# Rest rows of a gated MLP as pieces of the output stage, in an adaLN transformer block on one NeuronCore

## The chip, the core and the metric

The kernel runs on one core of a Trainium2 chip. Its engines work side by side: TensorE (PE, matrix products and transposes), VectorE (DVE), ScalarE (ACT), GpSimd (POOL) and SyncE (SP, which here only issues DMA transfers). Each engine takes its instructions in order, and so does each engine's queue of DMA issues. The metric is the device time of one execution in microseconds. Everything is float32.

## What is computed

One block with adaptive layernorm, for x of 2 batches x 1024 tokens x 1024 features, 32 heads of 32, and a gated MLP with 2752 inner rows:

```python
x = L0_attn_hidden_states
mod = (_silu(L0_c) @ L0_wmod).reshape(L0_c.shape[0], 6, 1, -1)
sa, ca, ga, sb, cb, gb = (mod[:, 0], mod[:, 1], mod[:, 2], mod[:, 3], mod[:, 4], mod[:, 5])
...
h = _layernorm(x, axis=-1) * (1 + ca) + sa
x = x + ga * _L0_attn_ref(h, L0_attn_Wqkv, ..., L0_attn_Wout)     # causal softmax with ALiBi
h = _layernorm(x, axis=-1) * (1 + cb) + sb
gate = jnp.einsum('bsh,ih->bsi', h, Wg) * ag
up = jnp.einsum('bsh,ih->bsi', h, Wu) * au
x = x + gb * (jnp.einsum('bsi,hi->bsh', jax.nn.silu(gate) * up, Wd) * ad)
```

## The kernel before

**Stages.** Modulation vectors and the layernorm of x; QKV projections of batch 0; attention of batch 0, then of batch 1, with dense products woven in; the rest of the output stage; gate and up; down. Large products are done with seven block products in place of eight (`seven`): the operands are sums of blocks, and what comes out is merged. For gate and up this is done at two levels, so the moving operands are sums T1 to T4 and blocks B11, B21, B22 of the second layernorm's output, over both batches, with inner sums of their own (`inner_b`, lines 1188 to 1202, four sums of 256 columns and four stores to `bop_dram`).

**Weaving.** `together(attention, dense_work(), share)` (line 1164) builds the program in the order in which the instructions will stand on each engine: it goes through attention's units (one block of scores, exponentials, products with V) and after each takes dense pieces until the planned microseconds of dense work reach `share(a)`. In batch 0's attention the dense work is the projections of batch 1, in batch 1's it is the output stage. The budgets are LEAD, DENSE0 and DENSE1 (line 1375).

**Output stage.** `output(b, js, ...)` (line 1285) goes pair by pair; a pair (b, j) is 256 tokens, j from 0 to 3. Its seven products of 4 matmuls 128x512 each use two PSUM banks in turn; VectorE and GpSimd gate them and add x. Then x1 is stored, the layernorm is done (`normalize`), four groups of transposes (`turned`, line 861) go through the `Todo` list, and h2, the transposed result, goes to DRAM. The list is worked off between the products of the next pair (from product `q0` on) and after them, and takes a bank of `banks.others`, which in attention is one bank.

**Rest rows.** Five stages of 512 rows leave inner rows 2560 to 2751. `rest_rows` (line 1396) does these 192 rows for each pair: three products of 8 matmuls with 256 columns (128 gate rows; 128 up rows; the last 64 of both in one), then Silu on ScalarE, one fused VectorE operation for the product with up, and a store to `rest_dram`.

**Between attention and gate** (lines 1558 to 1611): batch 0's h2 comes back from DRAM (`fetch`); rest rows of all eight pairs are done in twos, woven with the last transposes and with the output stage of pairs (1,2) and (1,3); `second(j)` makes the operands that need both batches: T1, T2, B22 on VectorE and T3, T4 on GpSimd. T3 and T2 share the tile `oo`.

**Gate and up.** Each of five stages (`for s in range(NSB)`) has seven entries (STAGES), each of seven block products into banks `gx`, `ux`, `gy`, `uy`. GpSimd makes the sums of weights (`gate_inner`, line 1700, and `gate_sums`, line 1691). `after(n, go)` (line 1737) puts work at a count of chain entries. `second_batch(3)` is made here (line 1744).

Of the kernel before, what the change touches and what calls it, by code (L numbers as in the profile page):

```python
# [18 lines left out]
P = 128  # L19
# [461 lines left out]
def kernel(  # L481
# [233 lines left out]

    last_exp = [None]
# [159 lines left out]
    class Todo:  # L876
# [18 lines left out]
        def add(self, go):  # L895
            self.list.append(go)

        def run(self, n, all_=False):
            self.place()
            for _ in range(min(n, len(self.list))):  # L900
                if not all_ and not self.banks.fresh():
                    return
                self.list.pop(0)(self.banks.turn())
                yield TURN
# [380 lines left out]
    def output(b, js, pools, banks, bt, todo, keep, q0=1):  # L1285
# [9 lines left out]
        for j in js:  # L1295
# [44 lines left out]
            for m in range(2):  # L1340
                for g in range(2):
# [10 lines left out]
                    todo.add(go)  # L1352

    def second_batch(j, pool, h0, h1):


        oo = pool.tile([P, 2, KC // 2, 2, P], FP, tag="oo", name=f"oo_{j}")
        t1, t4, lo1, hi1 = h0[:, 0 : KC // 2], h0[:, KC // 2 :], h1[:, 0 : KC // 2], h1[:, KC // 2 :]
        t2, t3 = oo[:, 0], oo[:, 1]
# [15 lines left out]
    LEAD, DENSE0, DENSE1 = 16.0, 370.0, 136.0  # L1375
# [20 lines left out]
    def rest_rows(pairs, rest_w, pool, psp, tiles):  # L1396

        n1 = REST[1][1]
        ib = 4 * NSB
        for b, j in pairs:  # L1400
            hl = tiles[b, j].rearrange("p k h t -> p k (h t)")
            ps = []
            for r in range(3):
                bank = psp.tile([P, 512], FP, tag="rp", name=f"rest_{b}_{j}_{r}")[:, 0:256]
                for k in range(KC):
                    matmul(bank, rest_w[r][:, k, :], hl[:, k, :], start=(k == 0), stop=(k == KC - 1))
                ps.append(bank)
                yield 3.4
            sg = pool.tile([P, 2, 256], FP, tag="rsg", name=f"rsg_{b}_{j}")
            ac = pool.tile([P, 2, 256], FP, tag="rac", name=f"rac_{b}_{j}")  # L1410
            nc.scalar.activation(sg[:, 0], ps[0], AF.Silu, scale=vt[:, R_AG + ib : R_AG + ib + 1])
            nc.scalar.activation(
                sg[64 : 64 + n1, 1], ps[2][0:n1], AF.Silu, scale=vt[0:n1, R_AG + ib + 1 : R_AG + ib + 2]
            )
            nc.vector.scalar_tensor_tensor(
                ac[:, 0], ps[1], vt[:, R_AU + ib : R_AU + ib + 1], sg[:, 0], ALU.mult, ALU.mult
            )
            nc.vector.scalar_tensor_tensor(
                ac[64 : 64 + n1, 1], ps[2][64 : 64 + n1],
                vt[64 : 64 + n1, R_AU + ib + 1 : R_AU + ib + 2], sg[64 : 64 + n1, 1], ALU.mult, ALU.mult,  # L1420
            )
            nc.sync.dma_start(rest_dram[0][:, b, j], ac[:, 0].rearrange("p (h t) -> p h t", h=2))
            nc.sync.dma_start(
                rest_dram[1][0:n1, b, j], ac[64 : 64 + n1, 1].rearrange("p (h t) -> p h t", h=2)
            )
# [93 lines left out]
    def dense_work():  # L1519
# [22 lines left out]
        out_args.extend((opools, banks, bt, Todo(banks), keep))  # L1542
        yield from output(0, range(NJ), *out_args)
        right["w"] = rest_weights(rwp, nc.sync)
# [15 lines left out]
    opools, _, bt, todo, _ = out_args  # L1560
# [5 lines left out]
    rps = rest_st.enter_context(tc.tile_pool(name="rest_ps", bufs=4, space=PSUM))  # L1566
# [7 lines left out]
    def rows(*pairs):  # L1574
        return rest_rows(pairs, rest_w, rest_pool, rps, kept)

# [4 lines left out]
    def with_turns(rows_):  # L1581

        together(rows_, todo.run(len(todo.list), True), lambda a: 0.16 * (a - 9.0))

    fetch(0, 0, nc.scalar)
    rest_w = right["w"]
# [7 lines left out]
    def between():  # L1594
        yield from rows((0, 1))
        second(0)
        yield from rows((1, 1))
# [472 lines left out]
```

## Time and profile before

| | |
|---|---|
| median of 3 executions | 2857.35 us (2853.57 to 2857.75) |
| the profiled execution's own time | 2851.89 us |
| its span, first to last instruction | 2850.2 us |
| granted TensorE clock, mean | 0.983 |
| batch 0's attention | about 388 to 901 us |
| batch 1's attention, first score block to last product with V | 901.4 to 1334.6 us |
| products of pair (1,2), start; of pair (1,3), end | 1382.98, 1454.93 us |
| last transposes of pair (1,3), end | 1480.2 us |
| gate, first product; end of stage 1 | 1501.43, 1553.35 us |

The span is cut into stretches by what TensorE works on. In a line of the windows the first number after the stretch is its length; then come the busy time of each engine with its instructions, the granted clock, the share of the DMA engines that is busy and what they move. A line of the waits names the waiting engine and tile, what the wait ended on, the sum, the number and the longest. A line of the timeline is start, length, engine, line, operation, output and input with their shapes, and in brackets the idle time ahead of it with what ended it. The chain of waits follows the last instruction back to what released it.

### The profile page before, as it was taken

What the parts mean: (1) busy time and instruction counts of PE and PEld (TensorE: products, weight loads), DVE (VectorE), ACT (ScalarE), POOL (GpSimd) and SP (SyncE); (2) the same over time, 40 slices, a digit from 0 to 9 for tenths busy, and PEclk for the clock granted to TensorE, in tenths of its full rate; (3) what the DMA queues carried; (4) which work ended last, traced back from release to release, by engine and by line L of the source; (5) the groups of instructions that cost most, each with busy time, mean ns of one, the idle gap of its engine ahead of it and who ended that gap; (6) DMA issues with size and microseconds to landing.
All of it is one profiled execution on the core that took longest, in us unless ns stands there. A gap on an engine that the chain in (4) does not pass through costs nothing. (4 is left out here: it accounts for less than half of the span.)

```text
span 2850.2 us, 29927 instructions
## 1 busy us (share of the span) xinstructions
PE 2698.4 (95%) x10271; PEld 1329.8 (47%) x10271; DVE 1454.4 (51%) x2285; ACT 685.5 (24%) x1523; POOL 1292.9 (45%) x1270
## 2 busy tenths in 40 slices
PE   7999999999999888889899999999999998999998
PEld 2444433333333222223664444444444447888776
DVE  5766525566634456656654453544535345443442
ACT  1322243444443556554111010110101101000000
POOL 3311124545565665655447474455636431322342
PEclk9999999999999899999999999999999999999999
DMA  9878873766755554433687576675866669554552
GB/s 348 301 278 296 293 241 107 237 225 201 233 157 191 155 172 137 149 123 113 198 295 252 162 265 195 192 271 162 272 183 229 201 190 279 150 148 137 167 143 79
DMA packets 377573, 579.14 MB, mean 203 GB/s; under 512 B 21590, under 2 KB 278712, under 8 KB 366276
## 3 DMA queue, kind: packets, MB, share of 16 engines
q1 hardware_dynamic: 363928, 556.12, 60.3%
q10 hardware_dynamic: 13484, 21.02, 2.3%
q8 instruction: 84, 1.38, 0.2%
q14 instruction: 77, 0.63, 0.1%
HBM read 411.89 MB, written 165.17 MB: 202 GB/s over the span
## 5 line engine op out<-in xcount | busy, mean ns | idle before, releaser
L1085 ACT ACTIVATE p<-sc,kw 128x128 f32<-128x128 f32 (+3 forms) x1024 | 421.6, 513 | 357.8 <-PE sc L763 341.7
L763 PE MATMUL bank<-wT,a 128*128 128x512 f32 x768 | 359.9, 613 | 12.0 <-DVE wT L832 6.8
L1117 POOL TENSOR_TENSOR p<-p,p 128x1024 f32<-128x1024 f32 (+3 forms) x128 | 262.4, 2050 | 174.6 <-PE av L763 142.6
L1117 DVE TENSOR_TENSOR p<-p,p 128x1024 f32<-128x1024 f32 (+3 forms) x192 | 250.2, 1314 | 142.8 <-POOL p L1089 85.0
L763 PE MATMUL bank<-wB,a 128*128 128x512 f32 x576 | 262.2, 601 | 1.2 <-DVE raw L984 0.6
L763 PE MATMUL sc<-cq,ck 32*128 32x512 f32 (+3 forms) x1536 | 192.9, 542 | 55.1 <-ACT p L1085 54.9
L763 PEld LDWEIGHTS bank<-wT,a 128*128 128x128 f32 x768 | 142.5, 195 | 189.8 <-issue 172.7
L1089 POOL TENSOR_SCALAR_AFFINE_SELECT p<-p 128x256 f32<-128x256 f32 x256 | 136.0, 544 | 196.2 <-ACT p L1085 192.5
L763 PE MATMUL av<-p,cv 128*32 128x512 f32 (+3 forms) x1536 | 170.6, 511 | 4.0 <-POOL p L1089 4.0
L763 PEld LDWEIGHTS bank<-wB,a 128*128 128x128 f32 x576 | 104.8, 190 | 144.3 <-issue 125.6
L763 PEld LDWEIGHTS sc<-cq,ck 32*128 32x128 f32 x1536 | 64.6, 186 | 192.2 <-ACT p L1085 106.3
L1842 PE MATMUL gy<-bt,sig 128*128 128x512 f32 x280 | 132.5, 596 | 10.9 <-DMA bt<-bop_B 6.0
L1842 PE MATMUL gx<-bt,sig 128*128 128x512 f32 x280 | 131.6, 592 | 0.0
L1842 PE MATMUL uy<-bt,siu 128*128 128x512 f32 x280 | 131.6, 592 | 0.0
L1842 PE MATMUL ux<-bt,siu 128*128 128x512 f32 x280 | 131.6, 592 | 0.0
L763 PEld LDWEIGHTS av<-p,cv 128*32 128x32 f32 x1536 | 33.8, 110 | 123.6 <-issue 81.5
L1842 PEld LDWEIGHTS gy<-bt,sig 128*128 128x128 f32 x280 | 52.4, 190 | 81.2 <-issue 71.3
L1842 PEld LDWEIGHTS uy<-bt,siu 128*128 128x128 f32 x280 | 53.2, 190 | 66.9 <-issue 66.0
L1842 PEld LDWEIGHTS gx<-bt,sig 128*128 128x128 f32 x280 | 53.2, 190 | 66.9 <-issue 66.1
L1842 PEld LDWEIGHTS ux<-bt,siu 128*128 128x128 f32 x280 | 53.2, 190 | 66.9 <-issue 65.0
L1842 PE MATMUL gx<-bt,wgS 128*128 128x512 f32 x160 | 75.2, 592 | 0.0
L1842 PE MATMUL ux<-bt,wuS 128*128 128x512 f32 x160 | 75.2, 592 | 0.0
(415 smaller groups left out, 4449.2 us busy)
## 6 DMA issues: line engine op xcount, KB each, us to landing
bt<-bop_T SPq DMA_DIRECT2D x140, 512.0 KB
bt<-bop_B SPq DMA_DIRECT2D x99, 512.0 KB
a<-hop SPq DMA_DIRECT2D x20, 1792.0 KB
wm<-in_L_wmod_dram SPq DMA_DIRECT2D x48, 512.0 KB
wB<-in_L_attn_Wqkv_dram SPq DMA_DIRECT2D x21, 1024.0 KB
aq_S<-act_S SPq DMA_DIRECT2D x16, 1280.0 KB
qk<-qs SPq DMA_DIRECT2D x16, 1024.0 KB
act_S<-asS SPq DMA_DIRECT2D x30, 512.0 KB
```

The lines of the kernel that those rows point to most:

```text
L763: return in_order(nc.tensor.matmul(*args, **kw_))
L1085: last_exp[0] = nc.scalar.activation(p[:, g, lo:hi], sp[:, g, lo:hi], AF.Exp, bias=kw[:, d, h_ : h_ + 1])
L1089: last_mask[0] = nc.gpsimd.affine_select(out=p[:, :, 0:P], in_=p[:, :, 0:P], pattern=[[0, 2], [1, P]], compare_op=ALU.is_ge, fill=0.0, bas ...
L1117: adders[b](half, jb).tensor_add(dst, dst, ps[half][:, :, 0:n])
L1842: nc.tensor.matmul(ps.rearrange("p (j t) -> p j t", j=NJ), ins[mat][qa][:, c2, :], bt[:, :, c2, :], start=(q in ("P1", "P2", "P5") and c2 ...
```

## The change

Rest rows are no longer a routine of their own after attention. `output` gets the rest weights and puts, behind a pair's transposes, three product pieces and two pieces without a planned cost (the activations) on its Todo list. In batch 1 the list is worked off from the sixth product on. DENSE1 rises from 136 to 190. Silu becomes g / (1 + exp(-g)), with the exponential on ScalarE (scale from the new constant `nag`) and the rest on VectorE; the up rows go through the constant-pool tile `sc`. Behind attention, three more PSUM banks join the shared one, batch 0's h2 is fetched on SP's queue, `second(0)` is done before the products of pair (1,2) and `second(1)` after those of (1,3); the operands of pairs 2 and 3 are both made in gate's first stages. T3 is made in place of the lower half of batch 1's h2, and `oo` holds T2 alone, in two buffers.

```diff
+    nag = const.tile([P, 2], FP, name="nag")
+    nc.vector.tensor_scalar_mul(nag, vt[:, R_AG + 4 * NSB : R_AG + 4 * NSB + 2], -1.0)
...
-        def add(self, go):
-            self.list.append(go)
+        def add(self, go, us=TURN):
+            self.list.append((go, us))
         def run(self, n, all_=False):
             self.place()
-            for _ in range(min(n, len(self.list))):
+            while n and self.list:
+                go, us = self.list[0]
+                if us is None:
+                    go()
+                    self.list.pop(0)
+                    continue
                 if not all_ and not self.banks.fresh():
                     return
-                self.list.pop(0)(self.banks.turn())
-                yield TURN
+                self.list.pop(0)
+                go(self.banks.turn())
+                n -= 1
+                yield us
...
-    def output(b, js, pools, banks, bt, todo, keep, q0=1):
+    def output(b, js, pools, banks, bt, todo, keep, q0=1, rest=None):
...
                     todo.add(go)
+            if rest is not None:
+                rest_pieces(b, j, todo, h2, *rest)
     def second_batch(j, pool, h0, h1):
-        oo = pool.tile([P, 2, KC // 2, 2, P], FP, tag="oo", name=f"oo_{j}")
+        t2 = pool.tile([P, KC // 2, 2, P], FP, tag="oo", name=f"oo_{j}", bufs=2)
         t1, t4, lo1, hi1 = h0[:, 0 : KC // 2], h0[:, KC // 2 :], h1[:, 0 : KC // 2], h1[:, KC // 2 :]
-        t2, t3 = oo[:, 0], oo[:, 1]
+        t3 = lo1
...
-    LEAD, DENSE0, DENSE1 = 16.0, 370.0, 136.0
+    LEAD, DENSE0, DENSE1 = 16.0, 370.0, 190.0
...
-    def rest_rows(pairs, rest_w, pool, psp, tiles):
...
+    def rest_pieces(b, j, todo, h2, rest_w, pool):
+        n1 = REST[1][1]
+        hl = h2.rearrange("p k h t -> p k (h t)")
+        tiles = {}
+        def product(w, bank):
+            ps = bank[:, 0:256]
+            for k in range(KC):
+                matmul(ps, w[:, k, :], hl[:, k, :], start=(k == 0), stop=(k == KC - 1))
+            return ps
+        def gate(ps, r, lo):
+            g, e = (pool.tile([P, 256], FP, tag=nm, name=f"{nm}_{b}_{j}_{r}") for nm in ("rg", "re"))
+            ib = R_AG + 4 * NSB + r
+            nc.scalar.activation(e[lo], ps[lo], AF.Exp, scale=nag[lo, r : r + 1])
+            nc.vector.tensor_scalar_mul(g[lo], ps[lo], vt[lo, ib : ib + 1])
+            tiles[r] = g, e
+        def act(r, lo, n):
+            g, e = tiles[r]
+            nc.vector.tensor_scalar(e[lo], e[lo], FAR, 1.0, ALU.min, ALU.add)
+            nc.vector.reciprocal(e[lo], e[lo])
+            nc.vector.tensor_mul(g[lo], g[lo], e[lo])
+            nc.vector.tensor_mul(g[lo], g[lo], urow[lo])
+            nc.sync.dma_start(rest_dram[r][0:n, b, j], g[lo].rearrange("p (h t) -> p h t", h=2))
+        every, lo, hi = slice(0, P), slice(0, n1), slice(64, 64 + n1)
+        urow = sc.rearrange("p k c -> p (k c)")
+        ib = R_AU + 4 * NSB
+        def up(bank):
+            nc.vector.tensor_scalar_mul(urow, product(rest_w[1], bank), vt[:, ib : ib + 1])
+        def last(bank):
+            ps = product(rest_w[2], bank)
+            gate(ps, 1, lo)
+            nc.scalar.activation(urow[lo], ps[hi], AF.Identity, scale=vt[hi, ib + 1 : ib + 2])
+        todo.add(lambda bank: gate(product(rest_w[0], bank), 0, every), 3.5)
+        todo.add(up, 3.5)
+        todo.add(lambda: act(0, every, P), None)
+        todo.add(last, 3.5)
+        todo.add(lambda: act(1, lo, n1), None)
...
+        out_args.append(1)
+        out_args.append((rest_weights(rwp, nc.sync), rwp))
         yield from output(0, range(NJ), *out_args)
-        right["w"] = rest_weights(rwp, nc.sync)
+        out_args[5] = 5
         yield from output(1, range(NJ // 2), *out_args)
...
-    rps = rest_st.enter_context(tc.tile_pool(name="rest_ps", bufs=4, space=PSUM))
+    rps = rest_st.enter_context(tc.tile_pool(name="rest_ps", bufs=1, space=PSUM))
+    banks.others = banks.others + [rps.tile([P, 512], FP, tag=f"rq{i}", name=f"rq{i}") for i in range(3)]
...
-    fetch(0, 0, nc.scalar)
-    rest_w = right["w"]
-    fetch(1, 0, nc.scalar)
     operands(1, NJ // 2, opools[1], wide)
     operands(1, NJ // 2 + 1, opools[1])
+    fetch(0, 0)
+    fetch(1, 0)
+    alone(todo.run(len(todo.list), True))
     fetch(0, 1)
-    with_turns(rows((0, 0), (1, 0)))
     fetch(1, 1)
-    def between():
-        yield from rows((0, 1))
-        second(0)
-        yield from rows((1, 1))
-    together(
-        between(), output(1, range(NJ // 2, NJ), *out_args, 3), lambda a: 0.6 * OUT_US / 2 * a / 20.6
-    )
-    in_range(rest_pool, rps)
+    second(0)
+    alone(output(1, range(NJ // 2, NJ), *out_args))
+    alone(todo.run(4, True))
     fetch(0, 2)
     second(1)
+    in_range(rest_pool, rps)
     fetch(0, 3)
-    with_turns(rows((0, 2), (1, 2)))
-    second(2)
-    alone(rows((0, 3), (1, 3)))
+    alone(todo.run(len(todo.list), True))
...
-            on_dve, on_pool = second_batch(3, pair_pool, kept[0, 3], kept[1, 3])
-            for go in on_dve[:2] + on_pool[:2]:
-                go()
-            for n, go in zip((8, 9, 12), on_dve[2:]):
+            on_dve, on_pool = [], []
+            for j in (2, 3):
+                d, p = second_batch(j, pair_pool, kept[0, j], kept[1, j])
+                for go in d[:2] + p[:2]:
+                    go()
+                on_dve += d[2:]
+                on_pool += p[2:]
+            for n, go in zip((2, 5, 6, 8, 9, 12), on_dve):
                 after(n, go)
-            for n, go in zip((10, 11), on_pool[2:]):
+            for n, go in zip((3, 4, 10, 11), on_pool):
                 after(n, lambda go=go: (go(), None)[1])
```

More of the change, by code (lines that the diff above doesn't have):

```diff
@@ L1394, in rest_weights @@
         return w
-    def rest_rows(pairs, rest_w, pool, psp, tiles):
+    def rest_pieces(b, j, todo, h2, rest_w, pool):
         n1 = REST[1][1]
[L1399 to L1413, printed above, removed]
-            )
[L1415 to L1425, printed above, removed]
@@ L1559 @@
     att.close()
-    opools, _, bt, todo, _ = out_args
+    opools, _, bt, todo = out_args[:4]
     pair_st = ctx.enter_context(ExitStack())
@@ L1572, in fetch @@
         eng.dma_start(kept[b, j], h2_dram[b][j])
-    def rows(*pairs):
-        return rest_rows(pairs, rest_w, rest_pool, rps, kept)
     def second(j):
@@ L1579, in second @@
             go()
-    def with_turns(rows_):
-        together(rows_, todo.run(len(todo.list), True), lambda a: 0.16 * (a - 9.0))
-    fetch(0, 0, nc.scalar)
-    rest_w = right["w"]
-    fetch(1, 0, nc.scalar)
     operands(1, NJ // 2, opools[1], wide)
     operands(1, NJ // 2 + 1, opools[1])
+    fetch(0, 0)
+    fetch(1, 0)
+    alone(todo.run(len(todo.list), True))
     fetch(0, 1)
-    with_turns(rows((0, 0), (1, 0)))
     fetch(1, 1)
-    def between():
-        yield from rows((0, 1))
-        second(0)
-        yield from rows((1, 1))
-    together(
-        between(), output(1, range(NJ // 2, NJ), *out_args, 3), lambda a: 0.6 * OUT_US / 2 * a / 20.6
-    )
-    in_range(rest_pool, rps)
+    second(0)
+    alone(output(1, range(NJ // 2, NJ), *out_args))
+    alone(todo.run(4, True))
     fetch(0, 2)
     second(1)
+    in_range(rest_pool, rps)
     fetch(0, 3)
-    with_turns(rows((0, 2), (1, 2)))
-    second(2)
-    alone(rows((0, 3), (1, 3)))
+    alone(todo.run(len(todo.list), True))
     ost.close()
```

## The prediction

> **What bounds the kernel now.** I read the page's busy times first, then the windows of the stages that the edit touches, the waits of TensorE in them, the timeline and last the chain of waits.
>
> ```profile
> PE 2698.4 (95%) x10271; PEld 1329.8 (47%) x10271; DVE 1454.4 (51%) x2285; ACT 685.5 (24%) x1523; POOL 1292.9 (45%) x1270
> ```
>
> TensorE bounds the whole kernel, so the questions are where it idles and whether the edit fills that idle time. The windows: batch 0's attention, batch 1's, two stretches of the output stage behind attention, the rows and transposes behind it, the first two gate stages.
>
> ```profile
> core 0: us, PE busy (x) PEld busy (x) DVE busy (x) ACT busy (x) POOL busy (x), PEclk, DMA share, GB/s
> 388.00:901.00 513.00, 496.41 (x2321) 185.55 (x2320) 271.07 (x412) 220.20 (x517) 260.20 (x267) 0.99 0.59 190
> 901.00:1335.00 434.00, 374.67 (x2174) 120.72 (x2176) 256.82 (x357) 241.70 (x580) 271.05 (x248) 0.94 0.48 149
> 1335.00:1383.00 48.00, 41.75 (x169) 29.71 (x170) 30.00 (x61) 4.58 (x9) 16.36 (x11) 0.96 0.70 216
> 1383.00:1455.00 72.00, 67.62 (x210) 37.72 (x209) 37.44 (x64) 9.63 (x15) 40.36 (x36) 1.00 0.74 239
> 1455.00:1501.00 46.00, 43.46 (x208) 37.49 (x207) 24.24 (x52) 8.45 (x12) 18.03 (x18) 1.00 0.82 277
> 1501.00:1553.00 52.00, 49.12 (x115) 21.41 (x114) 23.89 (x34) 5.66 (x11) 48.67 (x67) 1.00 0.78 245
> ```
>
> Batch 1's attention leaves TensorE idle for 434.0 - 374.7 = 59.3 us; behind attention, 1335 to 1501, it idles for 13.2 us of 166. Its waits in 901 to 1335:
>
> ```profile
> engine line waited for: us in total, times, longest us
> PE sc L763 <- ACT p L1085: 45.6, 42, 3.8
> PE bank L763 <- DVE h2t L869: 4.5, 1, 4.5
> ```
>
> The idle time is scores waiting for ScalarE's exponentials, in short pieces. Already one wait is for the VectorE eviction of the one PSUM bank that transposes share.
>
> The timeline has one pair's rest rows, and a reciprocal of 128 columns:
>
> ```profile
> 1348.49 10.52 PE L763 MATMUL rest<-hl,restw 128*128 128x256 f32 x48
> 1345.46 0.95 DVE L1138 RECIPROCAL rc<-rc 128x128 f32<-128x128 f32 x1 [2.88 <-DMA rc<-sum]
> ```
>
> The 48 records are one pair's 3 products of 8 matmuls, two records to a matmul: 10.35 us from start to start for a pair, 3.45 a product.
>
> The chain of waits ahead of gate, and POOL just ahead of the T3, T4 operands:
>
> ```profile
> 1463.98 6.13 DMA actr<-rac
> 1476.09 6.86 DMA bop_T<-inner_T
> 1492.21 4.93 DMA actr<-rac
> 1497.88 3.72 PE rest L763 x16
> ...
> 1510.41 2.35 POOL L1368 TENSOR_TENSOR hl<-hl,oo 128x1024 f32<-128x1024 f32 x1
> 1532.52 0.72 POOL L1698 TENSOR_TENSOR wuS<-wuA,wuS 128x256 f32<-128x256 f32 x1
> ```
>
> (The first four are the chain, the last two the timeline.) Stores and POOL operations set the order here, and rest rows are what TensorE does meanwhile.
>
> **What the Trainium skill says.** "ScalarE: Activation LUTs", What ACT_TABLE_LOAD costs: about 1283 ns for a load plus about 1380 ns of drain. The trace has loads of 1.28 us each; it does not show the drain apart. "VectorE: DVE Perf Modes", First, the fixed hardware budget: Reciprocal is an iterated divide with a repeat count of 8. The trace agrees in kind: 0.95 us beside 0.27 for a tensor_tensor of the same 128 columns. "SBUF — State Buffer", Who interferes with whom: a VectorE operation with two SBUF inputs contends with a GpSimd one that reads SBUF, for the whole instruction. The trace: 256-column operand sums of 0.41 us on VectorE, one taking 4.20 us at 1531.37 while POOL ran.
>
> **The change, part by part.**
>
> *Matmuls moved, none removed.* This and the places below are from the order of the built program. Rest rows are 8 x 10.35 = 83 us before and after. Of them (0,0) to (0,3), 12 products or 41.4 us, go into batch 1's attention. DENSE1 190 also asks for pair (1,1)'s last six half products there (10.3 us). Pairs (1,0) to (1,3) stay behind attention.
>
> *What they cost inside attention.* I measured the units of batch 1's attention, from one score block to the next. At 512 columns: 3.36 us with no dense piece (14 units), 4.38 with a 1.72-us piece (16), 5.38 with a piece and a transposition or settlement (14), 5.61 with two pieces (3). At 256: 2.40, 3.55, 5.47 with none, one and two. So a 1.72-us piece costs 1.0 to 1.15, a 3.45-us one 2.25 to 3.1. I take 2.6: 12 x 2.6 = 31, plus 6 x 1.05 = 6: **+37**. From below: if all 59.3 us of gaps were usable it would be nothing, but the gaps average 1.1 us each (45.6 in 42), so a 3.45-us product can't sit in one: at least 12 x 1.2 = 15. From above: nothing hidden is 51.7, and shared-bank waits like the 4.5 above can go past it.
>
> *VectorE.* A pair's activation was two 0.48-us operations, 0.97. Now: two multiplications out of PSUM (0.45 each), two min/add (0.25, from 0.22 for 128 columns), two reciprocals of 256 columns, four products (0.41, as the sums above) and `up` (0.45). The reciprocal is bounded by 0.95 (no more than 128 columns) and 1.9 (twice), and I take 1.9: 0.9 + 0.5 + 3.8 + 1.64 + 0.45 = 7.3. Four pairs add 29 us in attention, where none of it ran: 256.8 of 434 becomes 286 of 471, 61%. On average hidden behind TensorE; but VectorE runs in order, and the next piece needs its eviction, which I leave in the upper bound. Behind attention the same 7.3 stands between transposes and their bank; three added banks lighten that.
>
> *ScalarE's table loads* (seven between 1355 and 1465, 9 us) leave. ScalarE is busy 4.6 of 48 and 9.6 of 72 us there, so this is worth at most the 1.28 us on the chain at 1461.66: nothing on its own, since TensorE has rows to do.
>
> *From the end of batch 1's attention (1334.6) to the last transposes (1480.2).* Before: 145.6 us = 48.4 to the first product of pair (1,2), 72.0 for the two last pairs' products and two rows, 25.2 to the last transposition. After: the tail of (1,1), 13.9, is gone; its layernorm still takes the 13.7 from 1348.5 to the transposition at 1362.2, covered by 10.35 of rest (1,0); four transposes (0.66, with evictions about 7 in all), 10.35 of rest (1,1), and 7 for waits in the one bank with VectorE's evictions: about 39. Then 14 products x 3.44 = 48.2 plus about 5 for the transposes between them: 53. Then rest (1,2), 10.35, and four transposes: 14.6. Sum 107: **-38** (from -42, all waits gone, to -28).
>
> *From the last transposition to the end of gate's stage 1* (before: 1480.2 to 1553.35, 73 us, with 20.7 of rows ahead of gate). Ten us of rows leave. But a wait is added. second_batch(3), and now (2), run in gate's opening; T3, T4 are made in place, so POOL's T3 of pair 3 (`h2t_1_3`) must follow rest (1,3). POOL runs in order, and ahead of it stand 16 gate_inner operations, 32 gate_sums and hl_0_3: 48 x 0.683 + 2 x 2.35 = 37.5 us with itself (POOL was 94% busy in 1501 to 1553 already, and none of it can begin before the transposes free xr). SP's store bop_T3 waits for it, and behind that on SP stand T3, T4, B22, a bt load and last the rest store actr_1 of pair (1,3): ten issues of about 0.5, and 5 us for its landing (4.93 in the chain). ScalarE's first eviction of gate, whose tile takes the closed rest pool's space, waits for that store. Behind it on ScalarE stand all evictions of the stage, and TensorE's third chain entry waits for that bank. So entry 3 starts about 37.5 + 5 + 5 + 0.6 = 48 after the transposes, and from there to stage 1's end is 1508.3 to 1553.35 = 45 in the trace before, some 3 of it stalls that the later start covers: 48 + 42 = 90 against 73, **+17**. From below 0 (SP passes earlier and gate is bound by rows, whose 10 us then gain up to -10); from above +27, if weight loads queue behind.
>
> *New const, `nag`*: one small VectorE operation under the start's loads, 0.17 us without that cover. Fetches on SP rather than ScalarE: four issues of 0.5 in a queue that is waited for; in the bounds.
>
> **Sum.** 37 - 38 + 17 = +16. The profiled execution before took 2851.9 (span 2850.2 and 1.7 around it), so 2868; it lies 5.5 under the median of 2857.35, so as a median **2874**.
>
> **The rivals.**
> 1. *TensorE's gaps take the products* (other side). With VectorE and ScalarE at some 60%, products start while scores wait: 42 waits, 45.6 us. At an extension of 15, the sum is 15 - 38 + 17 = -6: 2851. It decides from an extension of 21 down. Against it: units with a piece are all longer. Chance 0.17.
> 2. *The wait at gate's start is short.* POOL or SP gets through, so gate starts some 12 us after the transposes: 37 - 38 - 5 = -6, 2851; if both, 2830. Chance 0.15. Against it: the counts above, and 48.67 of 52 us busy.
> 3. *VectorE and the shared bank bound attention.* Rest products, transposes and settlements all take one bank, and each waits for an in-order eviction: 12 x 4.5 = 54, sum 54 + 6 - 38 + 17 = +39, 2896. Chance 0.14.
> 4. *It does nothing:* 0 with opposite parts, inside 0.2%: about 2857.
>
> **How the numbers follow.** 0.2% is 5.7 us, about what can be told from no change. Likeliest case 0.54, its own range +5 to +32 (2862 to 2889), one in ten of it in the same band; rivals 1 and 2 together 0.32, of which some two thirds end faster than 5.7 under and most of the rest the same; rival 3 0.14. That gives faster 0.21, same 0.13, slower 0.66. Range 2846 to 2900: below it lies both good cases at once, above it bank waits and gate loads together.
>
> **What would show it.** Right: batch 1's attention 465 to 475 us long with TensorE busy above 88%; last attention product to last transposes about 107; ScalarE's first gate eviction ended by the store actr<-rg, and TensorE idle some 15 to 25 us in gate's third entry. Wrong: attention under 450, or no idle at gate's start, or waits for bank2's evictions above 20 us in attention.

## The result, and the profile after

The changed kernel takes 2905.78 us, median of 4 runs (2901.09 to 2910.17), beside 2855.46 us for the kernel before on the same chip: a ratio of 1.0169, with a 95% interval of 1.0149 to 1.0189. It is 50 us slower. The forecast was 2874 with a range up to 2900: right in its direction, 32 us too low, and the result lies outside the range.

The profiled execution has a span of 2908.4 us, 58.2 over that of before. The busy times on its page:

```profile
PE 2699.0 (93%) x10271; PEld 1331.4 (46%) x10271; DVE 1504.4 (52%) x2358; ACT 681.6 (23%) x1524; POOL 1291.8 (44%) x1270
```

TensorE's instructions are as many and its busy time the same within 1 us; VectorE has 50 us more. All that was lost is idle time of TensorE. The windows of the changed kernel, cut where those of before were cut: batch 1's attention; to the first product of pair (1,2); to the end of pair (1,3)'s products; to gate; gate's first two stages. ("Stage" is used here, as in the prediction, for one of the seven entries of STAGES, counted from 0, so the end of stage 1 is the end of the second. An "entry" of gate, the third or the seventh, is one of the seven block products in the first of them.)

```profile
core 0: us, PE busy (x) PEld busy (x) DVE busy (x) ACT busy (x) POOL busy (x), PEclk, DMA share, GB/s
897.00:1374.00 477.00, 423.13 (x2381) 159.99 (x2384) 290.72 (x402) 248.19 (x592) 268.61 (x251) 0.95 0.44 138
1374.00:1412.00 38.00, 29.46 (x138) 22.62 (x138) 27.22 (x63) 3.01 (x8) 4.71 (x4) 0.96 0.64 186
1412.00:1488.00 76.00, 51.17 (x124) 22.72 (x123) 45.51 (x69) 4.92 (x10) 48.35 (x38) 0.87 0.72 223
1488.00:1531.00 43.00, 28.35 (x119) 23.27 (x118) 32.75 (x62) 2.39 (x6) 22.57 (x23) 0.84 1.00 347
1531.00:1610.00 79.00, 49.88 (x114) 21.90 (x113) 27.55 (x47) 8.53 (x13) 48.44 (x63) 0.83 0.55 172
```

In attention TensorE idles for 53.9 us of 477, before for 59.3 of 434: it was given 49 us more to do, and only 5 of them came out of idle time. In the four windows behind it, TensorE idles for 77 us of 236; before it was 16 of 218. The granted clock has fallen there from 1.00 to between 0.83 and 0.87 in three of them.

By the anchors of the table of before (the first score block at 897.3, the last product with V at 1374.4, the last transposes' end at 1515.8, the end of gate's stage 1 at 1610.2):

| | before | forecast | measured |
|---|---|---|---|
| start of batch 1's attention | 901.4 | 0 | -4.1 |
| its length | 433.2 | +37 | +43.9 |
| from its end to the last transposes | 145.6 | -38 | -4.2 |
| from there to the end of stage 1 | 73.0 | +17 | +21.4 |
| sum | | +16 | +57.0 |

(The remaining 1.2 us of the span's 58.2 lie behind stage 1.) The earlier start is no gain of the change: in three runs below that differ from one another only behind attention (before_exp, exp_store_on_act, exp_pool_order) batch 1's attention starts at 891.9, 898.5 and 903.0 us. So stretches are compared by their length. One row holds 34 of the 41 us that were missed; attention holds 7, the stretch behind the transposes 4, and the early start gives 4 back. The waits of TensorE in batch 1's attention:

```profile
PE sc L766 <- ACT p L1096: 26.7, 27, 3.8
PE bank L769 <- DVE h2t L872: 9.7, 8, 2.7
PE bank L769 <- DVE rs L1138: 7.4, 2, 6.2
PE bank L766 <- issue: 4.1, 1, 4.1
```

And its three longest waits from the end of attention to the end of stage 1:

```profile
PE gx L1864 <- issue: 29.1, 1, 29.1
PE bank L766 <- DVE oP L1338: 21.9, 1, 21.9
PE rq L769 <- ACT sc L1449: 5.9, 1, 5.9
```

In attention the waits for exponentials fell from 45.6 to 26.7 us, and the waits of tile `bank` rose from 9.7 to 25.6 us, 21.2 of them in these lines. Behind it two single waits make 51 us.

**The wait of 29.1 us** is the forecast one, at gate's third entry. The changed kernel's timeline there, GpSimd, then SP, ScalarE and TensorE:

```profile
1554.66 2.34 POOL L1380 TENSOR_TENSOR h2t<-h2t 128x1024 f32<-128x1024 f32 x1
...
1557.03 1.57 SPq L1211 DMA_DIRECT2D bop_T<-h2t  x3
...
1561.99 0.45 SPq L1435 DMA_DIRECT2D actr<-rg  x1
...
1566.54 0.59 ACT L1663 COPY g_P<-gx 128x512 f32<-128x512 f32 x1 [31.51 <-DMA actr<-rg]
1567.22 3.61 PE L1864 MATMUL gx<-bt,sig 128*128 128x512 f32 x4 [29.12 <-issue]
```

T3 of pair 3 ends 41 us after the transposes (37.5 were worked out), the last rest store is issued 5 us later, and ScalarE's first gate eviction ends its wait 4.5 us after that.

**The wait of 21.9 us** was in no step of the forecast. The same kernel between the first and the second product of pair (1,3):

```profile
1438.96 3.60 PE L766 MATMUL bank<-wB_o,aoA 128*128 128x512 f32 x8
...
1456.66 0.42 DVE L1205 TENSOR_TENSOR inner_T<-hl 128x256 f32<-128x256 f32 x1 [6.03 <-POOL inner_T L1208]
1457.12 0.50 SPq L1314 DMA_DIRECT2D xr<-_attn_hidden_states_dram  x1
1460.14 0.43 DVE L1205 TENSOR_TENSOR inner_T<-oo 128x256 f32<-128x256 f32 x1 [1.92 <-DMA bop_T<-inner_T]
1462.45 1.26 POOL L1342 TENSOR_TENSOR xr<-xr,oP 128x512 f32<-128x512 f32 x1 [5.81 <-DMA xr<-_attn_hidden_states_dram]
1463.74 0.69 DVE L1338 TENSOR_TENSOR oP<-ga,bank 128x512 f32<-128x512 f32 x1 [2.05 <-POOL xr L1342]
1464.48 5.51 PE L766 MATMUL bank<-wB_o,aoA 128*128 128x512 f32 x8 [21.92 <-DVE oP L1338]
```

VectorE's eviction of the last product of (1,2) (line 1338) stands in its queue behind the operands of `second(0)` and `second(1)`. Those take turns with GpSimd's T3 and T4 in the two buffers of one tile, so VectorE waits for GpSimd's stores. And the load of x for this pair is issued by SP at 1457.12 only, behind the store of T4. By the brackets this load ended last: GpSimd's addition waits for it, and the eviction for GpSimd. VectorE's own queue was free 2.05 us before.

### The profile page after: what moved, and what is told of

It is laid out like the page before. It is cut to its first block, busy times and chain, and to the rows that moved or that the text cites. A ratio compares the mean times of both kernels' runs of the same rounds, so it can differ in the third digit from the quotient of the medians.

```text
span 2908.4 us, 29991 instructions
## 1 busy us (share of the span) xinstructions
PE 2699.0 (93%) x10271; PEld 1331.4 (46%) x10271; DVE 1504.4 (52%) x2358; ACT 681.6 (23%) x1524; POOL 1291.8 (44%) x1270
## 4 chain that ended last, share of the span: by engine, by line
PE 75%; DVE 7%; DMA 6%; issue 4%; POOL 4%; ACT 3%; SPq 0%; ACTq 0%; POOLq 0%; DVEq 0%
PE bank L766 24%; PE gx L1864 8%; PE ux L1864 8%; PE dx L1989 7%; PE gy L1864 6%; PE uy L1864 6%; PE dy L1989 5%; PE sc L766 5%; PE av L766 4%; ACT p L1096 3%; DVE p L1128 1%; DMA wm<-in_L_wmod_dram 1%; DMA xt<-_attn_hidden_states_dram 1%; PE bank L769 1%; DMA bt<-bop_B 1%
## 5 line engine op out<-in xcount | busy, mean ns | idle before, releaser
L766 PEld LDWEIGHTS bank<-wB,a 128*128 128x128 f32 x576 | 104.5, 190 | 145.6 <-issue 124.6
L1864 PE MATMUL gx<-bt,sig 128*128 128x512 f32 x280 | 133.3, 599 | 29.1 <-issue 29.1
L766 PE MATMUL bank<-wB_o,aoA 128*128 128x512 f32 x128 | 66.8, 654 | 26.0 <-DVE oP L1338 21.9
L766 PE MATMUL bank<-h2t,restw 128*128 128x256 f32 x272 | 68.4, 408 | 9.5 <-DVE h2t L872 6.0
```

The costliest lines, as they stand in the source:

```text
L766: return in_order(nc.tensor.matmul(*args, **kw_))
L1864: nc.tensor.matmul(ps.rearrange("p (j t) -> p j t", j=NJ), ins[mat][qa][:, c2, :], bt[:, :, c2, :], start=(q in ("P1", "P2", "P5") and c2 ...
```

## The experiments

### The wait at gate: order on GpSimd

```diff
-                for go in d[:2] + p[:2]:
+                for go in d[:2]:
                     go()
+                t_ins = [go() for go in p[:2]]
...
-                        nc.gpsimd.tensor_add(o["S1"], o["S3"], o["A22"])
+                        first = nc.gpsimd.tensor_add(o["S1"], o["S3"], o["A22"])
+                        if t_ins:
+                            for t_ in t_ins:
+                                behind(first, t_)
```

> The changed kernel, with GpSimd's T4 and T3 of pair 3 put ahead of gate's weight sums, so that they no longer stand behind 32 sums. My reading (ScalarE's first gate eviction waits for the last rest store, which waits on SP behind T3): T3 can then end about 2.4 us after the last rest rows, the store is issued about 5 us later and lands 5 us after that, so gate's third entry starts about 13 us after the last rest rows and not 36: 18 to 25 us less than the changed kernel's 2905.8, about 2884. Rival (weight loads, or the bt transfers, are late there anyway): less than 8 us gained, and another releaser in the same place.

Measured: 2894.34 us (ratio to before 1.0127, 1.0092 to 1.0161), 11.4 less than the changed kernel's 2905.78. The third entry starts 13.75 us after the last rest rows (1543.59 after 1529.84), as worked out, so the chain of T3, SP and the store is what held it. The gain is less than the 18 to 25 us expected. Of the 22 us by which TensorE's wait at the third entry falls (29.1 to 6.7), 11 reach the end. The profile puts the 6.7 us down to a weight sum, but this product does not read that sum; ScalarE's first gate eviction still waits for the same store and ends just ahead of it:

```profile
1542.90 0.59 ACT L1663 COPY g_P<-gx 128x512 f32<-128x512 f32 x1 [8.92 <-DMA actr<-rg]
1543.59 3.75 PE L1869 MATMUL gx<-bt,sig 128*128 128x512 f32 x4 [6.72 <-POOL wgS L1717]
```

A further 5.1 us are waited for at the seventh entry, where VectorE's eviction stands behind an operand that waited 17.3 us for the store of another operand.

### The wait behind attention: two chains that end together

`own_tile` gives GpSimd's inner operands a buffer of their own; the second run adds the queue of the x loads.

```diff
-        t_ = pool.tile([P, 4, 2, P], FP, tag="inner", name=f"inner_{o}_{j}", bufs=2)
+        t_ = pool.tile([P, 4, 2, P], FP, tag="inner" if eng is nc.vector else "innerp", name=f"inner_{o}_{j}",
+            bufs=2 if eng is nc.vector else 1)
...
-                nc.sync.dma_start(xr, x[b, ts(qts[m], P), :])
+                (nc.scalar if b == 1 and j >= NJ // 2 else nc.sync).dma_start(xr, x[b, ts(qts[m], P), :])
```

> The changed kernel, with GpSimd's inner operands in a tile of their own, so that VectorE no longer waits for GpSimd's T3 and T4 stores of pair 0 ahead of its eviction of the last product of pair (1,2). Reading A, two chains end within 2 us of each other there (this one, and the load of x for pair (1,2), which SP issues only behind the T4 store): at most 5 us gained, and the 21.9 us of TensorE waiting stay at 15 or more. Reading B, the tile alone is the cause: about 20 us gained, about 2886.

> The same with the loads of x for pairs (1,2) and (1,3) on ScalarE's queue instead of SP's, so that neither chain is left. Reading A: the 21.9 us of TensorE waiting fall under 5, and 15 to 22 us are gained over the changed kernel, about 2887. Rival (the operands of pair 0 and 1 and their stores are only late by then, and the wait moves to the layernorm and transposes of (1,2) and (1,3)): under 8 us gained.

Measured: 2901.23 us (1.0160, 1.0127 to 1.0192) with the tile alone, 4.6 less than the changed kernel and, by the intervals, not clear of nothing; 2889.77 (1.0130, 1.0091 to 1.0169) with both, 16.0 less. The wait for the eviction is 5.1 us then. Reading A holds: the tile alone leaves 15.2 us of the wait, and both together take most of it. The load of x moved alone was not run; by the trace it could have gained some 2 us there, until VectorE's queue was the last.

All three edits together, with an inner tile, a queue and an order of GpSimd's operations:

> The changed kernel with all three edits of the runs before: T3, T4 ahead of gate's weight sums, an inner tile of GpSimd's own, and x loads of the last two pairs on ScalarE's queue. If the two waits lie behind one another and share nothing, the gains add: 11.5 + 16 = 27, about 2879. If one takes over what the other gave: at most 20 gained, 2886 or more. Either way it stays over the kernel before by 20 us or more, since the loss in attention and of cover is not touched.

Measured: 2882.65 us (1.0085, 1.0060 to 1.0109), 23.1 less: between the two readings, nearer to the sum (27). It is still 24 us over the kernel before.

### What the rest rows were worth behind attention

The kernel before, with seven of eight matmuls of batch 0's rest products left out where they stand behind attention, and nothing moved in its source:

```diff
-                for k in range(KC):
-                    matmul(bank, rest_w[r][:, k, :], hl[:, k, :], start=(k == 0), stop=(k == KC - 1))
+                for k in range(KC if b else 1):
+                    matmul(bank, rest_w[r][:, k, :], hl[:, k, :], start=(k == 0), stop=(k == (KC if b else 1) - 1))
```

> The kernel before, with the rest rows of batch 0 where they were, behind attention, but of each of their 12 products only the first of eight matmuls: 36 of 41.4 us of TensorE's work are left out, and the values are not the reference's. If they are cover (layernorms, operands and stores set the time there): 8 to 22 us less than before, about 2841. If TensorE sets the time there: 30 to 36 less, about 2822.

Measured: 2856.81 us, a ratio of 1.0002 (0.9991 to 1.0013). **36 us of TensorE's work taken away, and nothing gained**: less than even the cover reading had expected. Its waits of TensorE from the end of attention to gate show what stands in their place:

```profile
PE bank L766 <- DVE xr L747: 35.0, 2, 22.0
PE bank L766 <- DVE h2t L869: 4.5, 3, 2.9
PE rest L763 <- DVE rac L1415: 4.2, 1, 4.2
```

Two waits of transposes for VectorE's layernorm take 35.0 us; in the kernel before the same wait was 4.4. But the matmuls are not all that differs. The build placed VectorE's operations in another order. The kernel before at pair (1,1):

```profile
1360.27 2.60 DVE L747 TENSOR_SCALAR xr<-xr,mv_f,rstd_f 128x1024 f32<-128x1024 f32 x2 [3.85 <-DMA x<-xr]
1362.20 0.66 PE L766 MATMUL bank<-ident,xr 128*128 128x128 f32 x4 [3.19 <-DVE xr L747]
1362.69 3.70 PE L763 MATMUL rest<-hl,restw 128*128 128x256 f32 x9
1363.18 1.21 DVE L1361 TENSOR_TENSOR hl<-hl,hl 128x1024 f32<-128x1024 f32 x1
```

And this kernel there:

```profile
1361.17 1.23 DVE L1361 TENSOR_TENSOR hl<-hl,hl 128x1024 f32<-128x1024 f32 x1 [3.42 <-DMA hl<-h]
1373.60 1.53 DVE L747 TENSOR_SCALAR xr<-xr,mv_f,rstd_f 128x1024 f32<-128x1024 f32 x2
1374.47 1.11 PE L766 MATMUL bank<-ident,xr 128*128 128x128 f32 x4 [22.00 <-DVE xr L747]
```

The operands of `second(0)` (line 1361 and what follows it) stand behind this layernorm in the kernel before and ahead of it here; on ScalarE, Silus and their table loads stand ahead of it too. From the last product of (1,1) to the transposition it is 13.7 us before and 23.5 here, so some 10 of the 36 us went to the new order. At pair (1,3) it is 11.8 and 14.6. The run shows that this stretch, as built, gets no shorter without the rows: the layernorms, with what stands ahead of them on VectorE, now take times that the rows had covered. What the kernel before would gain without the rows and with its own order was not measured.

### What they cost inside attention

Moved alone: the kernel before, with only batch 0's rest rows as pieces in batch 1's attention.

```diff
-    LEAD, DENSE0, DENSE1 = 16.0, 370.0, 136.0
+    LEAD, DENSE0, DENSE1 = 16.0, 370.0, 178.0
...
-        yield from output(0, range(NJ), *out_args)
         right["w"] = rest_weights(rwp, nc.sync)
+        yield from output(0, range(NJ), *out_args, rest=(right["w"], rwp))
...
-    with_turns(rows((0, 0), (1, 0)))
+    with_turns(rows((1, 0)))
...
-        yield from rows((0, 1))
+        yield 10.3
...
-    with_turns(rows((0, 2), (1, 2)))
+    with_turns(rows((1, 2)))
...
-    alone(rows((0, 3), (1, 3)))
+    alone(rows((1, 3)))
```

> The kernel before, with nothing changed but that the rest rows of batch 0 (12 products, activation by the exponential as in the change) are pieces of the output stage in batch 1's attention; DENSE1 is 178, which adds just their planned 42 us, so the rest of the output stage stays where it was. Reading A (attention pays 38 to 42 us for 41 us of matmuls, and behind attention about as much goes): between 6 us less and 12 us more than before, about 2860. Rival (moving the rows is itself the loss, since what they covered behind attention now shows): 25 us or more above before.

Measured: 2880.81 us (1.0088, 1.0055 to 1.0120), 27 more than before: the rival. Attention takes 480.1 us and not 433.2: 47 more for 41 us of moved matmuls. The stretch from its end (1375.65) to the last transposes is 142.7 us and not 145.6, although 31 us of rows have left it, and the rest up to stage 1's end gains 13.4. A line of the timeline shows the cover gone, a transposition that waits for its layernorm:

```profile
1490.25 10.53 PE L766 MATMUL rest<-h2t,restw 128*128 128x256 f32 x48
1509.47 1.08 PE L769 MATMUL bank<-ident,xr 128*128 128x128 f32 x4 [8.69 <-DVE xr L750]
```

Two variants of this kernel ask what attention pays for. In the first, all of the activation but the first reading of the banks is left out:

```diff
-            nc.vector.tensor_scalar(e[lo], e[lo], FAR, 1.0, ALU.min, ALU.add)
-            nc.vector.reciprocal(e[lo], e[lo])
-            nc.vector.tensor_mul(g[lo], g[lo], e[lo])
-            nc.vector.tensor_mul(g[lo], g[lo], urow[lo])
```

> As the kernel before with batch 0's rest rows in batch 1's attention, but of their activation only the first reading of the banks is left (exponential, two scalings, the copy of the up rows): min and add, reciprocals and products are left out, 5.9 us of VectorE per pair; their values are not those of the reference. If attention pays for the matmuls (their 3.45 us each show in full): within 8 us of the 2880.8 with activation, and attention still some 470 us long. If it pays for VectorE's activation ahead of the evictions of the shared bank: 15 us or more less, attention at 460 or less.

Measured: 2876.94 us (1.0070, 1.0047 to 1.0094), 3.9 less, attention 2.7 us shorter. This part of VectorE's activation is not what attention pays.

In the second, seven of eight matmuls of each moved product are left out:

```diff
-            for k in range(KC):
-                matmul(ps, w[:, k, :], hl[:, k, :], start=(k == 0), stop=(k == KC - 1))
+            matmul(ps, w[:, 0, :], hl[:, 0, :], start=True, stop=True)
```

> The kernel with batch 0's rest rows in batch 1's attention (2880.8; attention 480 us), with only the first of each product's eight matmuls: 36 us of TensorE's work left out, values not the reference's, pieces, evictions and activations as they were. If attention pays for the matmuls themselves: 28 to 38 us less, about 2847, attention some 447 us. If it pays for the handing over of the one shared bank and for evictions: under 15 us less, attention over 465.

Measured: 2869.73 us (1.0044, 1.0025 to 1.0062), 11.1 less, and attention takes 466.2 us, 13.9 less: the second reading, and against mine. Of 36 us of matmuls attention absorbs 22. But it is still 33 us longer than before with nearly all of the products' work gone. Its waits in attention:

```profile
PE sc L766 <- ACT p L1096: 42.5, 44, 3.8
PE bank L769 <- DVE xr L750: 7.6, 3, 4.8
PE bank L769 <- DVE h2t L872: 7.3, 7, 2.0
PE bank L766 <- ACT sc L1479: 5.0, 1, 5.0
PE bank L766 <- DVE h2t L872: 4.5, 2, 3.2
PE bank L766 <- issue: 4.1, 1, 4.1
PE bank L766 <- DVE rg L1456: 3.2, 1, 3.2
```

The waits of tile `bank` sum to 31.7 us; in the kernel before there were 9.7 in all. That is 22 of the 33, and the waits for exponentials are 3 less. The remaining 14.6 us are busy time of TensorE; the eighth of the products that is left accounts for 5 of them, and the granted clock of the stretch is 0.92, where it was 0.94. The pieces stand in a chain on one bank: layernorm, transposition, eviction to h2, rest product that reads this h2, eviction, next piece. Before, no matmul in attention read h2. Whether the one bank or the chain through h2 makes the waits was not separated: no run gives attention a second bank.

### Silu from the exponential

The kernel before, with this part alone (exponential, VectorE's min, add, reciprocal and products in `rest_rows`, rows where they were):

```diff
-            nc.scalar.activation(sg[:, 0], ps[0], AF.Silu, scale=vt[:, R_AG + ib : R_AG + ib + 1])
...
+                nc.scalar.activation(se[p_, r], ps_[p_], AF.Exp, scale=nag[p_, r : r + 1])
...
+                nc.vector.tensor_scalar(se[p_, r], se[p_, r], FAR, 1.0, ALU.min, ALU.add)
+                nc.vector.reciprocal(se[p_, r], se[p_, r])
```

> The kernel before with the Silu of the rest rows made of the exponential as in the change (table loads gone, 6.3 us more of VectorE per pair), the rows where they were. If both are hidden behind attention by the rows themselves: within 5 us of before. If VectorE's activations hold up layernorms and transposes: 8 us or more slower. If the table loads were on the path: 4 us or more faster.

Measured: 2880.12 us (1.0085, 1.0061 to 1.0109), 21 more. I had held it to be hidden. TensorE waits 27.1 us at gate's third entry, with no operand moved into gate. I took it for the same chain as in the changed kernel, the last rest store on SP, and moved that store:

```diff
-            nc.sync.dma_start(
+            (nc.scalar if (b, j) == (1, NJ - 1) else nc.sync).dma_start(
                 rest_dram[1][0:n1, b, j], ...
```

> The kernel before with the rest rows' Silu made of the exponential (2880, with 27.1 us of TensorE waiting at gate's third entry), and the last rest store issued by ScalarE's queue instead of SP's; nothing else differs. If that store's place on SP behind T3 is the cause: the wait falls under 8 us and the time to 2854 to 2864. If the wait belongs to what is late on SP in any case (bt of entry 7 stands there too): under 10 us gained, and the idle time is some entries later.

Measured: 2879.07 us (1.0073, 1.0054 to 1.0092), the wait still 27.0. So not this store's place on SP. The timeline of the kernel with the exponential alone tells another chain:

```profile
1521.39 0.72 POOL L1200 TENSOR_TENSOR inner_T<-oo,inner_T 128x256 f32<-128x256 f32 x1
1522.15 1.23 DVE L1365 TENSOR_TENSOR oo<-h2t,hl 128x1024 f32<-128x1024 f32 x1 [16.42 <-POOL inner_T L1200]
1525.95 0.83 ACT L1417 ACTIVATE rse<-rest,nag 128x256 f32<-128x256 f32 x2 [21.79 <-DVE rsg L1424]
1534.87 0.47 ACT L1420 ACTIVATE rac<-rest,vt 64x256 f32<-64x256 f32 x1 [8.09 <-DMA actr<-rac]
1535.37 0.58 ACT L1649 COPY g_P<-gx 128x512 f32<-128x512 f32 x1
```

In the built program GpSimd's inner operand of pair 2 has come to stand behind gate's 32 weight sums. VectorE, in order, waits 16.4 us for it, ScalarE's exponentials of the last pair's rows wait for VectorE, ScalarE's reading of the up rows then waits 8.1 us for a store of rest rows, and the gate eviction stands behind that on ScalarE. So in the next run the sums go behind the last operand of `second(2)`, and with it behind the others:

```diff
-                        nc.gpsimd.tensor_add(o["S1"], o["S3"], o["A22"])
+                        first = nc.gpsimd.tensor_add(o["S1"], o["S3"], o["A22"])
+                        for t_ in t_ins:
+                            behind(first, t_)
```

> The kernel before with the exponential form of the rest rows' Silu (2880, 27.1 us of waiting at gate's third entry), with gate's first weight sums put behind GpSimd's operands of pair 2 and T3, T4 of pair 3; SP's store is as it was. If the wait is GpSimd's 32 sums ahead of operands that VectorE and, behind it, ScalarE wait for: the wait falls under 8 us and the time to 2853 to 2866. If it is VectorE's longer activation itself: under 8 us gained.

Measured: 2865.30 us (1.0029, 1.0019 to 1.0040), 14.8 less than with the exponential alone; the wait at the third entry is 8.5 us, a little over the bound that was set. (The profile names a weight sum here too, which this product does not read; ScalarE's gate eviction ends just ahead of it, behind 6.4 us of waiting for a store of rest rows.) GpSimd's order is most of the 21 us. The 7.6 us left against before are this 8.5 or VectorE's activation; it wasn't separated.

The other way round, the changed kernel with ScalarE's Silu kept:

```diff
-            nc.scalar.activation(e[lo], ps[lo], AF.Exp, scale=nag[lo, r : r + 1])
-            nc.vector.tensor_scalar_mul(g[lo], ps[lo], vt[lo, ib : ib + 1])
+            nc.scalar.activation(e[lo], ps[lo], AF.Silu, scale=vt[lo, ib : ib + 1])
...
-            nc.vector.reciprocal(e[lo], e[lo])
...
```

> The changed kernel with the rest rows' activation by ScalarE's Silu again and one product on VectorE (25 table loads more than before, 1.28 us each, 16 of them in attention; 6.3 us less of VectorE per pair). In the built program the last rest store then stands on SP ahead of T3 of pair 3. If the exponential's longer VectorE chain is what put that store behind T3, the 29 us of TensorE waiting at gate's third entry go; attention pays up to 20 us for table loads: 2876 to 2896, about 2887. If the stall came of the moved operands of pair 2, it stays, and the run is at 2906 or above.

Measured: 2903.60 us (1.0155, 1.0135 to 1.0175), outside what was expected, and no different from the changed kernel. The 29.1 us at the third entry are 1.9, as expected of the order on SP, but the wait has moved:

```profile
PE gx L1860 <- DMA bt<-bop_B: 13.4, 1, 13.4
```

The bt of the seventh entry still stands on SP behind T3. And attention is 12.2 us longer than in the changed kernel (489.2 beside 477.0), although VectorE has less to do: 24 table loads run in it (1.28 us each, 30.8 together), 8 more than I had counted, since the layernorms' two need theirs too. The Trainium skill ("ScalarE: Activation LUTs", What ACT_TABLE_LOAD costs) gives about 2.66 us for a switch with its drain; this trace leaves no room for the drain (the load at 1064.74 begins 0.02 us behind the operation before it, and the next operation 0.01 us behind the load), so a switch is about 1.3 us here. The 24 loads come with 12.2 us of attention's length, 0.5 each; that ScalarE has slack in part of the units is argued, not shown. So inside attention the exponential was worth its place; over the whole kernel the two forms come out the same.

With the own tile and the x loads on ScalarE's queue as well:

> The changed kernel with Silu kept, and with GpSimd's own inner tile and the x loads of the last two pairs on ScalarE's queue. With both waits gone what is left is attention's 44 us for moved work, against the about 15 to 20 us saved behind attention and 10 at gate: about 2871, from 2862 to 2880; still slower than before. If moving the rows is harmless once the waits are gone: 2857 or less.

Measured: 2897.45 us (1.0136, 1.0117 to 1.0155): a miss. The last transposes end 13.8 us earlier than with Silu alone, but TensorE waits 17.9 us for the same bt and 3.4 for another: nearly all is given back there.

### Filling attention otherwise

```diff
-    LEAD, DENSE0, DENSE1 = 16.0, 370.0, 136.0
+    LEAD, DENSE0, DENSE1 = 16.0, 370.0, 150.0
```

> The kernel before with DENSE1 150 in place of 136 and nothing else: the last products of pair (1,1), 13.9 us behind attention, go into it. If they fit the idle time there in part: 3 to 9 us faster than before. If attention pays them in full: within 3 us of before.

Measured: 2855.35 us, 0.9990 (0.9979 to 1.0002): at most 0.2% gained, and not clear of nothing. Attention takes 445.6 us, 12.4 more, so it pays most of the 13.9 us of products. Products of one matmul at a time on top of that:

```diff
-            yield from seven(lambda q, i: a[q][:, i, :], bt, banks, read, todo.places(q0, 1, ahead), 2)
+            yield from seven(lambda q, i: a[q][:, i, :], bt, banks, read, todo.places(q0, 1, ahead), 1)
```

> The kernel before with DENSE1 150 and the output stage's products given to attention in pieces of one matmul (0.86 us) instead of two, so that more units get one. If the idle time in attention is bound to units without a piece: 4 to 12 us faster than before. If it belongs to the chain from scores to exponentials in every unit: within 4 us of before.

Measured: 2876.81 us (1.0063, 1.0048 to 1.0079), 21 slower, outside both readings. Beside before_dense150, which has the same products in attention, waits for exponentials fell from 35.4 to 28.1 us, but waits for VectorE's evictions to h2 rose from 8.6 to 17.8: the same exchange as in the change, with nothing left over. Attention takes 458.6 us, 13.0 more again, and this is no idle time (55.1 us beside 57.2): TensorE is busy 15.0 us longer for the same products in smaller pieces. Why stays open. No version here beats the kernel before beyond doubt.

## Why the prediction was wrong

**"Now from the end of attention to the last transposes: -38" is the step that failed.** It measured -4.2 (its own terms make -39, 39 + 53 + 14.6 = 106.6 of 145.6). In the changed kernel the three terms can be read one by one. To the first product of (1,2) it is 37.4 us, where 39 was worked out: right. From there to the end of (1,3)'s products (1488.5) it is 76.7, not 53. From there to the last transposes it is 27.3, not 14.6. So two terms failed.

The first, 24 us short, left out the wait of 21.9 us for operands, their stores and the load of x, with the slow product behind it: I had followed `second_batch` in gate, where it was new, and not `second(0)` and `second(1)` around the last products, where they now stand ahead of VectorE's evictions and SP's loads of x. With most of that wait away (own_tile_x_on_act) this term is 57.0 and the stretch 127.0 us, though its first term has grown there to 43.2.

The second, 13 us short, took the layernorm of (1,3) to be covered by 10.35 us of rest rows. The changed kernel, from the first product of (1,2) and from the last of (1,3):

```profile
1411.76 7.03 PE L766 MATMUL bank<-wB_o,aoA 128*128 128x512 f32 x16
...
1486.60 1.88 PE L766 MATMUL bank<-wT_o,aoA 128*128 128x512 f32 x4
1499.59 1.74 DVE L1432 RECIPROCAL re<-re 128x256 f32<-128x256 f32 x1
1502.92 3.68 DVE L750 TENSOR_SCALAR xr<-xr,mv_f,rstd_f 128x1024 f32<-128x1024 f32 x2
1506.03 1.09 PE L769 MATMUL rq<-ident,xr 128*128 128x128 f32 x4 [4.46 <-DVE xr L750]
1514.68 1.12 PE L769 MATMUL rq<-ident,xr 128*128 128x128 f32 x4 [5.86 <-ACT sc L1449]
```

From there to the first transposition it is 17.6 us; in the kernel before it was 11.8. The activation of rest rows (1,2) and the operands of pair 2 now stand between the layernorm's steps on VectorE. The last transposes then wait 5.9 us for a bank, whose rest product's activation waits in turn for a store of rest rows to be done with VectorE's tile. The prediction had seen the 7.3 us of VectorE's activation "between transposes and their bank" and put down no time for them here, since three added banks "lighten that". The kernel before idles for 13 us in 145 here, and I took TensorE for the limit. rows_eighth_behind says the same from the other side, with the reserve that its VectorE queue was ordered otherwise: a stretch in which TensorE is 91% busy got no shorter without 36 us of its work.

**Attention, +37**: +43.9, at 477 us just outside the 465 to 475 that would have shown it right. In its working it was wrong, and that the size came out near is in part luck. "A 3.45-us piece costs 2.25 to 3.1" came of units with other pieces; by rows_eighth_attention (batch 0's rows moved alone) the matmuls of a product cost about 1.3 us (13.9 us for 12 of them less an eighth), so rival 1, the gaps, took some 60% of them. Most of the rest is waiting for the one bank, as in rival 3, here joined by rest products that wait for h2: two rivals that I weighed against each other happened together. The upper bound of 51.7 held.

**Gate, +17**: +21.4, and its chain was right link by link: T3 behind the sums, SP, the store, ScalarE's first eviction. The third entry starts 51.4 us after the last transposes, where 48 was worked out: T3 ends 41 us after them and not 37.5. The other microsecond is less than the slow product behind the wait (1.7 us, below), which was left out.

**VectorE**: 34 us more in attention, where 29 were worked out; the reciprocal took 1.75 us where I took 1.9. Of ScalarE's table loads between 1355 and 1465 the trace of before has eight and not seven. **Silu at nothing on its own**: wrong. I judged the activations by their busy time; before_exp shows 21 us, of which 15 are an order on GpSimd that the longer chain brought with it. Within the changed kernel this order can't be told apart from that of the moved operands.

**The sum**: +16 against +57; 34 of the 41 us missed are the one step, 7 attention, 4 gate, and 4 come back from the early start. **The chances**: faster and same got 0.34. Waits at several places at once were named only as what lies above the range, and in no rival; that is what came.

## What to carry to other kernels

Before work is moved out of a stretch, ask what its time would be without that work: take most of it away and measure, as rows_eighth_behind does, since busy filler looks like a bound. Then see from the timelines whether the engines' queues kept their order, because leaving work out can change it. Compare stretches by their length, not by where they end. Work that is moved to fill gaps must not share a bank and a chain of dependences with what is there; price the handing over, not only the matmuls. And every operation with a wait inside it is to be followed on each in-order queue that it is put ahead of: here GpSimd's sums, VectorE's operands and SP's stores made three waits of 16 to 29 us.

## What was not expected of the hardware

TensorE was slow for a few microseconds after most of its longer waits. In the changed kernel the product behind the 21.92 us wait took 5.51 us for what takes 3.60 elsewhere, and the one behind 29.12 us took 3.61 in place of 1.88. So 1.7 to 1.9 us come on top of each of these waits; in gate_order, behind 6.72 us, two products together took 2.8 us more. With the rows of batch 0 moved alone, the transposition behind 8.69 us of waiting took 1.08 in place of 0.60, as did the three behind it, each with a pause of its own.

A short wait can do it too, and its effect can set in later. After the 3.19 us of waiting at 1362.20 in the kernel before, the transposition took 0.66, but of the rest products behind it nine records took 3.70 us, and sixteen such take 3.62 elsewhere. The granted clock shows the spell:

```profile
1363.20:1366.20 3.00, 3.00 (x9) 2.37 (x8) 2.96 (x5) 0.00 (x0) 0.42 (x1) 0.50 0.26 70
```

In exp_pool_order a wait of 2.75 us (at 1429.14) was followed by a product of 5.40 us for 3.60; in the kernel before one of 3.43 us (at 1443.26) by none that was slower. The Trainium skill ("TensorE: Matmul & The Clock Gate", Part 1: The HAM clock gate) says that the clock falls to half after an idle window of about 3.4 us, and is whole again after as long a busy one. The half clock and the length of the spell agree (some 3.3 us, and half of that is the 1.7 that was seen); 3.4 us of waiting as the least that brings it on do not come out of these runs. A forecast that adds a wait of some 3 us or more should add about 2 us to it, as an estimate from these cases.
